# A two-layer decoder on one core: eight sequences in flight instead of seven, in shared tiles, and three projection biases moved from TensorE to GpSimd

## The chip, the cores and the metric

The kernel runs on one core of a Trainium2 chip. The time is the device time of one launch in microseconds (us), the median of several runs. Engines are named as the profile names them: PE is TensorE (PEld its weight loads), DVE is VectorE, ACT is ScalarE, POOL is GpSimd and SP is SyncE, which here only issues transfers. One execution is also recorded by the hardware profiler; its span runs from the first to the last instruction.

## The reference: what is computed

Sixteen independent sequences (B = 16) of 128 tokens with 256 features pass through two decoder layers. Each layer is self-attention, cross-attention and a feed-forward part, each followed by a layer norm. In short:

```python
x = layernorm(x + L0_attn(x))            # 16 heads, RoPE in a latent space of 32, causal softmax, c_proj + bias
x = layernorm(x + L0_xattn(ctx, x))      # linear attention: q @ (k^T v) * scale, then (.+x) layer norm with gamma, beta
x = layernorm(x + L0_ffn(x))             # FP4-quantised gate/up/down with silu, hidden 704
x = layernorm(x + L1_attn(x))            # causal softmax attention plus a second, moving-average term; proj + bias
x = layernorm(x + L1_xattn(x, ctx))      # masked softmax attention, Wo + bo, norm, relu MLP of 1024, norm
x = layernorm(x + L1_ffn(x))             # FP6-quantised linear layer + bias
```

Everything is float32. Three of these biases concern the change: that of c_proj in the first self-attention ("cproj"), bo in the second cross-attention ("x1o"), and that of the last linear layer ("f1"). Each is a row of 256 numbers that is added to every token's output.

## The kernel before

One sequence at a time fits all engines: its 128 tokens are the 128 partitions. The whole chain for one sequence is a Python generator, `stages(b, s)`, that runs `l0_attn`, `l0_xattn`, `l0_ffn`, `l1_attn`, `l1_xattn` and `l1_ffn` in turn. Here `b` is the sequence (an "entry") and `s = b % NS` is its slot. `NS = 7` slots exist, so seven entries are in flight at once; entry `b + 7` takes the slot of entry `b` when that is done. While the weights are being quantised, at the start, the last slot is lent to them (`quantised_weights`, released under "place"), and a few tiles of slots 4 and 5 hold start-up data.

Every slot has tiles of its own in SBUF, made by `mine(s, tag, ...)`: four large ones, A, B, C and D, used again and again by the steps of an entry; "yT" for transposed activations and for the sums ahead of a layer norm; and two "x" tiles that alternate (`turn`), for the running activations and, at first, the transposed input. Shared by all slots are the PSUM tiles: one group of four banks ("s", `quad`) for scores and four single banks ("p", `bank`), and the work tiles "e" (4), "t2" (3), "bd" (1), "silu", "fc" and others.

The order of instructions on every engine is fixed while the program is built, by a planner. Each generator yields what its next step needs: an engine, buffers and tiles. The class `Clock` keeps a modelled time per engine and tile, and at every turn of the last loop (`while runs`) the planner lists the entries whose next step could start within 0.05 us of the earliest. Of these it takes the one with the lowest key: entries that hold PSUM or work tiles first, then by the time at which the step became ready plus a constant `DELAY` of that entry, rounded to steps of 8 us, and then the older entry. Within a step, instructions are emitted to all engines that it uses, so each engine's queue is the planner's order. A transfer is issued by SP, in order, and waits in its queue until its tile is free.

When a PE step would start later than PE is free by at least `LEAST = 0.8` us, `Timed.fill` issues matmuls on constants ("filler", 128 x 512 in bf16), as many as fit into `SHARE = 0.75` of the gap, each counted as 0.222 us:

```python
        for _ in range(int(SHARE * gap / cost)):
            c.run("PE", bank, (), cost, 0.17)
            self._e.matmul(bank, lhsT=lhsT, rhs=rhs, start=True, stop=True)
```

A bias row is added on PE: `bias_row` multiplies a selecting matrix `sel` with a tile `bt` that holds the biases split into three bf16 terms, as the first matmul of an accumulation; `product` then adds the real matmuls. `out_proj` does a projection, and VectorE adds the residual x while it reads the PSUM bank. Sums of x and a row that a later step needs are made by GpSimd in `with_bias`, from `rows`, a tile in which a row is repeated in every partition. In the kernel before, this serves "x0b" and "be2".

All engine instructions are recorded in the profile under line 208 (a wrapper), fillers under line 161; so groups are told apart by tile names. For instance `ps_op_a<-bt,sel` is a bias row of an output projection, and `xb_be` is a sum made by `with_bias`.

Of the kernel before, what the change touches and what calls it, by code (L numbers as in the profile page):

```python
# [17 lines left out]
NS = 7  # L18
# [6 lines left out]
SHARE, LEAST = 0.75, 0.8  # L25

DELAY = (3.07, 2.06, 3.48, 0.32, 3.35, 1.80, 2.92, 0.82, 1.65, 1.28, 1.58, 3.49, 2.27, 4.62, 2.80, 1.07, 0.06)
# [9 lines left out]
    ("x0kv", 2 * D), ("cproj", D), ("a1p", D), ("x1o", D), ("x1b2", D), ("x1v", H * VW), ("f1", D), ("l2o", H * VW),  # L37
    ("x0g", D), ("x0b", D), ("g1", D), ("be1", D), ("g2", D), ("be2", D),
]
NADD = 3 * 512 + 2 * H * VW + D  # L40

BIASES = [
    ("x0kv", 0, 0, 512), ("cproj", 1, 0, D), ("a1p", 1, D, D), ("x1o", 2, 0, D), ("x1b2", 2, D, D),
    ("x1v", 3, 0, H * VW), ("f1", 3, H * VW, D),
]
NB = H * VW + D
# [167 lines left out]
def decoder_kernel(ctx: ExitStack, tc: tile.TileContext, a: dict, out: bass.AP):  # L214
# [13 lines left out]
    turns = {}  # L228

    def turn(name, n):  # L230
        turns[name] = turns.get(name, -1) + 1
        return turns[name] % n

# [18 lines left out]
    def mine(s, tag, shape, name, dtype=F32):  # L252

        return ring(own, f"{tag}{s}", 1, shape, dtype, name)
# [23 lines left out]
    def load_input(b):  # L278

        s = b % NS  # L280
        t = mine(s, f"x{turn(f'x{s}', 2)}_", [P, 2, P], f"xT_in_{b}")
        nc.sync.dma_start(out=t, in_=a["xT"][:, :, b * T : (b + 1) * T])
        if b < 3:
            clock.load(t, 8 * P)
        else:
            arrives(t)
        incoming[b] = t
# [22 lines left out]
    for g in range(4):  # L310
        n = 512 if g < 3 else NB
        nc.scalar.dma_start(
            out=brow[32 * g : 32 * g + 3, :n], in_=a["rows"][:, 512 * g : 512 * g + n].partition_broadcast(3)
        )
    clock.load(brow, 4 * 512 * 12 // P, True)
# [48 lines left out]
    sel = const.tile([P, 4, P], BF16, tag="sel", name="sel")  # L364
    V.tensor_copy(sel, group.unsqueeze(2).to_broadcast([P, 4, P]))
# [8 lines left out]
    for i in range(0, 5, 2):  # L374
        n = min(2, 5 - i)
        cm = wk.tile([P, 2, 64], F32, tag="bd", name="cm", bufs=1)
        GP.memset(cm, 0.0)
        GP.affine_select(
            out=cm, in_=cm, compare_op=ALU.is_ge, fill=-1e30, base=96 - 64 * i, pattern=[[-64, 2], [-1, 64]],
            channel_multiplier=1,  # L380
        )
        GP.tensor_copy(causal[:, i : i + n, :], cm[:, :n, :])
# [42 lines left out]
    l2o = own.tile([P, H * VW], F32, tag="B5", name="l2o")  # L425
# [91 lines left out]
    def new_x(b, s, name):  # L517

        k = turn(f"x{s}", 2)
        return mine(s, f"x{k}_", [P, D], f"x_{name}_{b}")  # L520
# [28 lines left out]
    def product(p, lhsT, weight, name):  # L549

        bias_row(p, name)
        n = lhsT.shape[1]
        for c in range(n):
            PE.matmul(p, lhsT=lhsT[:, c, :], rhs=weight[:, c, :], start=False, stop=(c == n - 1))
# [130 lines left out]
    def features(y, s, name):  # L685

        yT = mine(s, "yT", [P, 2, P], f"yT_{name}")
        yield from transposed(y, 2, yT, name)
        return yT

    def out_proj(yT, weight, bias, residual, s, name):

        yield "PE", "p", yT
        p = bank((D,), f"op_{name}")
        product(p, yT, weight, bias)
        yield "V", p
        h = mine(s, "yT", [P, D], f"h_{name}")
        V.tensor_tensor(h, p, residual, ALU.add)
        return h

# [54 lines left out]
    def fold_values():  # L755
        yield "PE", "p"
        t = bank((4, P), "fold_t")
        for kc in range(2):
            for oc in range(2):
                PE.transpose(t[:, 2 * kc + oc, :], raw_v[:, kc, oc * P : (oc + 1) * P], ident)  # L760
        yield "S", t
        vT = own.tile([P, 4, P], F32, tag="B4", name="fold_vT")
        S.copy(vT, t)
        yield "PE", "p"
        t = bank((P,), "fold_k")
        PE.transpose(t, w["w_kv2l"], ident)
        yield "S", t
        kT = own.tile([P, P], F32, tag="D4", name="fold_kT")
        S.copy(kT, t)
        yield "PE", "p"  # L770
        p = bank((4 * VW,), "fold_m")
        PE.matmul(p, lhsT=kT, rhs=raw_l2o, start=True, stop=True)
        yield "S", p

        m = own.tile([P, 8 * VW], F32, tag="A4", name="fold_md")
        GP.memset(m, 0.0)
        S.copy(m[:64, : 4 * VW], p[:64, :])
        S.copy(m[64:, 4 * VW :], p[64:, :])
        for kc in range(2):
            yield "PE", "p"  # L780
            p = bank((H * VW,), f"fold_w{kc}")
            for oc in range(2):
                PE.matmul(
                    p[:, oc * 8 * VW : (oc + 1) * 8 * VW], lhsT=vT[:, 2 * kc + oc, :], rhs=m, start=True, stop=True
                )
            yield "S", p
            S.copy(wv[:, kc, :], p)
        yield "PE", "p"
        p = bank((H * VW,), "fold_b")
        for oc in range(2):  # L790
            PE.matmul(
                p[:, oc * 8 * VW : (oc + 1) * 8 * VW], lhsT=col("qkv", 4 + oc).to_broadcast([P, P]), rhs=m,
                start=True, stop=False,
            )
            for i in range(2):
                at = (2 * oc + i) * 4 * VW
                PE.matmul(
                    p[:, at : at + 4 * VW], lhsT=col("kv2l").to_broadcast([P, P]), rhs=raw_l2o, start=False, stop=(i == 1)
                )
        yield "V", p  # L800
        V.tensor_tensor(l2o, p, l2o, ALU.add)
        yield from three_terms(bl, l2o, H * VW)
        release("wv", [bl, wv])
# [33 lines left out]
    def l0_attn(b, s):  # L837
# [13 lines left out]
        q = mine(s, "B", [P, 4, P], f"q0_{b}")  # L851
# [21 lines left out]
        yield "PE", "p", rot  # L873
        p = bank((4, P), f"qfk_{b}")
        PE.matmul(p, lhsT=w["w_wqk"], rhs=rot, start=True, stop=True)
        yield "S", p
        S.activation(q, p, AF.Identity, bias=wqk_b, scale=LAT**-0.5)
        ctx_ = context(b, s, "0")
# [5 lines left out]
        S.copy(v[:, : H * VW], p)  # L884
        y = yield from attention(b, s, q, k, v, None, f"a0_{b}", "A")
        yield "PE", "bt", y
        yT = yield from features(y, s, f"a0_{b}")
        h = yield from out_proj(yT, w["w_cproj"], "cproj", xs[b], s, f"a0_{b}")
# [5 lines left out]
    def l0_xattn(b, s, ctx_):  # L894
# [6 lines left out]
        xT = yield from features(xs[b], s, f"x0_{b}")  # L901
# [12 lines left out]
        yield "V", "bd", p2  # L914
        bd = work("bd", 1, [P, 2, P], f"bd_{b}")
# [6 lines left out]
        h = mine(s, "yT", [P, D], f"h_x0_{b}")  # L922
        V.tensor_tensor(h, p3.rearrange("p a b -> p (a b)"), xs[b], ALU.add)
        xb = with_bias(b, s, "x0b", "A")
        z = mine(s, "C", [P, D], f"z_x0_{b}")
# [59 lines left out]
    def l0_ffn(b, s):  # L985
# [3 lines left out]
        qT = yield from features(q, s, f"xq_{b}")  # L989
# [31 lines left out]
        r = mine(s, "yT", [P, D], f"h_f0_{b}")  # L1021
# [5 lines left out]
    def l1_attn(b, s):  # L1027
        xT = yield from features(xs[b], s, f"x1a_{b}")
# [3 lines left out]
        qa = mine(s, "A", [P, 2, P], f"a1qa_{b}")  # L1032
        ka = mine(s, "D", [P, 4, P], f"a1ka_{b}")
# [11 lines left out]
        project(p, w["w_a1k2"], xT)  # L1045
        yield "S", p
# [11 lines left out]
        ahead = mine(s, "yT", [P, D], f"ahead_{b}")  # L1058
# [46 lines left out]
        yT = mine(s, "yT", [P, 2, P], f"yT_a1_{b}")  # L1105
        S.copy(yT, p)
        h = yield from out_proj(yT, w["w_a1p"], "a1p", xs[b], s, f"a1_{b}")
# [5 lines left out]
    def l1_xattn(b, s, ctx_):  # L1113
# [25 lines left out]
        xT = yield from features(xs[b], s, f"x1_{b}")  # L1139
# [6 lines left out]
        yT = yield from features(y, s, f"x1y_{b}")  # L1146
        h = yield from out_proj(yT, w["w_x1o"], "x1o", xs[b], s, f"x1_{b}")
        t = mine(s, "C", [P, D], f"x1_{b}")
        yield from layernorm_affine(t, h, "g1", row("be1"), f"x1i_{b}")
        tT = yield from features(t, s, f"x1t_{b}")  # L1150
# [17 lines left out]
        h = mine(s, "yT", [P, D], f"h_ff_{b}")  # L1168
# [7 lines left out]
    def l1_ffn(b, s):  # L1176
        yield "V", xs[b]
        if b + NS < B:
            load_input(b + NS)
        q = mine(s, "D", [P, D], f"f1q_{b}")  # L1180
        yield from fp6(q, xs[b], D, f"f1_{b}")
        qT = yield from features(q, s, f"f1_{b}")
        h = yield from out_proj(qT, wf, "f1", xs[b], s, f"f1_{b}")
        y = mine(s, "C", [P, D], f"out_{b}")
        yield from layernorm(y, h, f"f1_{b}")
        nc.sync.dma_start(out=out[b], in_=y)
# [13 lines left out]
    places.update((tag, (tag, 1)) for tag in ("fc", "fC", "silu", "bd", "mT", "mi", "mb"))  # L1200
# [80 lines left out]
    while runs:  # L1281
        able = [(r.start(), r.age, r) for r in runs]
        able = [r for r in able if r[0] is not None]
        first = min(r[0] for r in able)


        at, _, run = min(
            (r for r in able if r[0] <= first + 0.05),
            key=lambda r: (not r[2].held, round((r[2].ready + DELAY[int(r[1]) if r[1] >= 0 else B]) / 8.0), r[1]),
        )  # L1290
        run.step(at)
        if run.need is None:
            runs.remove(run)
# [116 lines left out]
```

## Time and profile before

| | before |
|---|---|
| median of 3 runs | 985.59 us (984.91 to 986.45) |
| the profiled execution, its own time | 988.3 us |
| its span, first to last instruction | 986.6 us |
| mean granted TensorE clock | 0.983 |
| PE busy | 919.7 us, 11965 matmuls |
| DVE busy | 700.7 us |
| ACT busy | 508.8 us |
| POOL busy | 432.2 us |
| fillers on PE | 182, 44.5 us |

The page gives busy time by engine, the span in 40 slices of about 24.7 us (a digit is tenths of busy time; PEclk is the clock granted to TensorE, in tenths of full speed), groups of equal instructions with their number, total and mean time and the idle time of the engine ahead of them, and the waits. The mean of a PE instruction is a latency: matmuls are pipelined, and the next one starts before the last is out.

### The profile page before, as it was taken

How to read it: one execution, taken by the hardware profiler on the slowest of the kernel's cores; microseconds unless marked ns; L12 is line 12 of the kernel's file. 1: busy time of each engine (PE TensorE's matmuls, PEld its weight loads, DVE VectorE, ACT ScalarE, POOL GpSimd, SP SyncE). 2: the span in 40 equal slices, each digit the busy share in tenths (PEclk: the TensorE clock that was granted, in tenths of full speed). 3: DMA queues.
4: the chain of work that ended last, by engine and by line, in shares of the span. 5: the costliest groups of instructions: out<-in, count | busy, mean ns of one | idle time of the engine just before them, and what ended most of it. 6: DMA issues, size and time to landing. Idle time of an engine off the chain costs nothing.

```text
span 986.6 us, 28364 instructions
## 1 busy us (share of the span) xinstructions
PE 919.7 (93%) x11965; PEld 723.2 (73%) x11965; DVE 700.7 (71%) x1440; ACT 508.8 (52%) x1113; POOL 432.2 (44%) x898
## 2 busy tenths in 40 slices
PE   7889899999899999999999999999998899999996
PEld 6566567777678878788777787878776687686764
DVE  5999999976764666659596967957666458963544
ACT  3244445665556444655546666555555545555432
POOL 3335523644435344445363464435434435344321
PEclk9899999999999989999999999999999999999998
DMA  8910000000000000000000000000000000000000
GB/s 230 210 45 7 28 7 7 11 9 20 5 23 12 19 25 21 23 22 17 18 18 16 21 13 7 24 1 23 21 13 25 8 11 7 14 13 15 10 7 12
DMA packets 47864, 25.57 MB, mean 26 GB/s; under 512 B 23004, under 2 KB 45516, under 8 KB 47480
## 3 DMA queue, kind: packets, MB, share of 16 engines
q1 hardware_dynamic: 46816, 22.39, 8.3%
q8 instruction: 94, 1.54, 0.6%
q0 software_dynamic: 192, 0.93, 0.4%
q10 hardware_dynamic: 728, 0.44, 0.1%
q14 instruction: 34, 0.28, 0.1%
HBM read 19.57 MB, written 2.10 MB: 22 GB/s over the span
## 4 chain that ended last, share of the span: by engine, by line
PE 55%; DVE 26%; ACT 8%; POOL 6%; issue 4%; DMA 0%; ACTq 0%; POOLq 0%; DVEq 0%
PE ps_ff L208 10%; PE ps_s_a L208 3%; PE ps_dn L208 3%; PE ps_st_a L208 3%; DVE nm_a L208 3%; DVE rope L208 2%; PE ps_op_a L208 2%; PE ps_x0kv L208 2%; PE ps_pg L208 2%; PE ps_pu L208 2%; PE ps_a1qk L208 2%; PE ps_yt L208 2%; DVE hh L208 2%; PE ps_qk L208 2%; PE ps_st_x L208 2%
## 5 line engine op out<-in xcount | busy, mean ns | idle before, releaser
L208 POOL TENSOR_SCALAR_AFFINE_SELECT e_a<-e_a 128x1024 f32<-128x1024 f32 x64 | 76.0, 1190 | 88.9 <-ACT e_a L208 88.7
L208 DVE TENSOR_REDUCE nm_a<-ps_s_a 128x16 f32<-128x2048 f32 x32 | 73.1, 2286 | 28.4 <-PE ps_s_a L208 28.2
L208 ACT ACTIVATE e_a<-ps_st_a 128x1024 f32<-128x1024 f32 x64 | 65.7, 1030 | 27.1 <-PE ps_st_a L208 26.9
L208 PE MATMUL ps_ff<-yT_x1t,w 128*128 128x128 f32 x512 | 63.1, 277 | 1.0 <-ACT yT_x1t L208 1.0
L208 PEld LDWEIGHTS ps_ff<-yT_x1t,w 128*128 128x128 f32 x512 | 60.1, 192 | 4.4 <-issue 2.1
L208 PE MATMUL ps_ff<-w,ff 128*128 128x256 f32 x256 | 61.0, 381 | 0.0
L208 ACT ACT_TABLE_LOAD x41 | 52.6, 1283 | 12.8 <-DMA brow<-in_rows_dram 9.0
L208 POOL CAST maxima<-nm_a 128x16 bf16<-128x16 f32 x32 | 8.9, 279 | 98.8 <-DVE nm_a L208 98.8
L208 PEld LDWEIGHTS ps_ff<-w,ff 128*128 128x128 f32 x256 | 46.2, 190 | 7.7 <-ACT ff L208 1.0
L208 ACT ACTIVATE ff<-ps_ff,cols 128x128 f32<-128x128 f32 x128 | 36.5, 369 | 27.1 <-PE ps_ff L208 27.0
L208 PE MATMUL ps_dn<-qw_down,hT 128*128 128x256 f32 x192 | 47.2, 383 | 0.7 <-ACT hT L208 0.5
L208 PE MATMUL ps_pg<-gu,yT_xq 128*128 128x352 f32 x128 | 44.7, 471 | 0.7 <-DVE hh L208 0.4
L208 DVE TENSOR_REDUCE nm_x<-ps_s_x 128x16 f32<-128x2048 f32 x16 | 36.5, 2282 | 11.4 <-PE ps_s_x L208 11.1
L161 PE MATMUL ps_filler<-ones,ident_b 128*128 128x512 bf16 x182 | 44.5, 383 | 0.0
L208 PE MATMUL ps_pu<-gu,yT_xq 128*128 128x352 f32 x128 | 43.2, 460 | 0.6 <-DVE bd L208 0.6
L208 PE MATMUL ps_yp_a<-e_a,v_a 128*32 128x128 f32 x1024 | 36.5, 281 | 3.6 <-POOL e_a L208 2.3
L208 ACT ACTIVATE e_x<-ps_st_x 128x1024 f32<-128x1024 f32 x32 | 31.8, 1026 | 13.7 <-PE ps_st_x L208 13.7
L208 PEld LDWEIGHTS ps_dn<-qw_down,hT 128*128 128x128 f32 x192 | 34.4, 190 | 5.6 <-ACT hT L208 0.7
L208 POOL TENSOR_SCALAR_AFFINE_SELECT maT<-maT 128x1024 f32<-128x1024 f32 x16 | 18.0, 1123 | 42.0 <-ACT maT L208 42.0
L208 ACT ACTIVATE x_x<-z_x,rstd_x 128x256 f32<-128x256 f32 x32 | 19.3, 604 | 31.7 <-POOL rstd_x L208 26.8
L208 ACT ACTIVATE x_a<-h_a,rstd_a 128x256 f32<-128x256 f32 x32 | 19.4, 605 | 31.4 <-POOL rstd_a L208 29.9
L208 PEld LDWEIGHTS ps_yp_a<-e_a,v_a 128*32 128x32 f32 x1024 | 26.3, 111 | 12.0 <-issue 4.8
(367 smaller groups left out, 2659.2 us busy)
## 6 DMA issues: line engine op xcount, KB each, us to landing
ctx<-in_ctxT_dram SPq DMA_DIRECT2D x32, 128.0 KB
xT_in<-in_xT_dram SPq DMA_DIRECT2D x16, 128.0 KB
w<-in_w_dram SPq DMA_DIRECT2D x2, 1024.0 KB
x_in<-in_x_dram SPq DMA_DIRECT2D x16, 128.0 KB
out_dram<-out SPq DMA_DIRECT2D x16, 128.0 KB
ahead<-x_f SPq DMA_DIRECT2D x16, 127.0 KB
mi<-in_mask_dram SPq DMA_DIRECT2D x16, 64.0 KB
rows<-in_rows_dram POOLq DMA_DIRECT2D x1, 768.0 KB, 5.5
```

The source lines that it names most:

```text
L161: self._e.matmul(bank, lhsT=lhsT, rhs=rhs, start=True, stop=True)
L208: return f(*args, **kw)
```

## The change

`NS` becomes 8. To make room for eight sets of tiles, "yT", the second "x" tile and the shared "bd" go: the input lands in B, transposed activations and sums go to whichever of A to D is free at that step (`features` and `out_proj` now take the tag), `ahead` takes the second half of the tile that holds `qa`. In `l0_attn` the product for v is done ahead of the one with `w_wqk`, since q is to take the place of the transposed input. The slots lent at the start change with it (slot 7 for the weights, slot 6 for `fold_values`).

The biases of "cproj", "x1o" and "f1" leave `bt` and join `rows`. `with_bias` adds each to x on GpSimd in the step ahead of the projection; `out_proj_onto` does the projection without a bias row, and VectorE adds PSUM onto that sum in place. The bias "a1p" stays on PE.

In the planner, `LEAST` becomes 1.4, the `DELAY` values are smaller (0.04 to 0.56), and the key is rounded to 2 us instead of 8.

```diff
-NS = 7
+NS = 8
...
-SHARE, LEAST = 0.75, 0.8
-
-DELAY = (3.07, 2.06, 3.48, 0.32, 3.35, 1.80, 2.92, 0.82, 1.65, 1.28, 1.58, 3.49, 2.27, 4.62, 2.80, 1.07, 0.06)
+SHARE, LEAST = 0.75, 1.4
+
+DELAY = (0.04, 0.26, 0.15, 0.27, 0.15, 0.52, 0.34, 0.45, 0.56, 0.30, 0.28, 0.08, 0.47, 0.04, 0.22, 0.10, 0.51)
...
-    ("x0kv", 2 * D), ("cproj", D), ("a1p", D), ("x1o", D), ("x1b2", D), ("x1v", H * VW), ("f1", D), ("l2o", H * VW),
+    ("x0kv", 2 * D), ("a1p", D), ("x1b2", D), ("x1v", H * VW), ("l2o", H * VW), ("cproj", D), ("x1o", D), ("f1", D),
     ("x0g", D), ("x0b", D), ("g1", D), ("be1", D), ("g2", D), ("be2", D),
 ]
-NADD = 3 * 512 + 2 * H * VW + D
+NADD = 2 * 512 + 2 * H * VW
...
     def load_input(b):
 
         s = b % NS
-        t = mine(s, f"x{turn(f'x{s}', 2)}_", [P, 2, P], f"xT_in_{b}")
+        t = mine(s, "B", [P, 2, P], f"xT_in_{b}")
...
     def new_x(b, s, name):
 
-        k = turn(f"x{s}", 2)
-        return mine(s, f"x{k}_", [P, D], f"x_{name}_{b}")
+        return mine(s, "x", [P, D], f"x_{name}_{b}")
...
-        bias_row(p, name)
+        if name is not None:
+            bias_row(p, name)
...
+    def out_proj_onto(h, yT, weight, name):
+
+        yield "PE", "p", yT, h
+        p = bank((D,), f"op_{name}")
+        product(p, yT, weight, None)
+        yield "V", p, h
+        V.tensor_tensor(h, p, h, ALU.add)
...
-        yield "PE", "p", rot
-        p = bank((4, P), f"qfk_{b}")
-        PE.matmul(p, lhsT=w["w_wqk"], rhs=rot, start=True, stop=True)
-        yield "S", p
-        S.activation(q, p, AF.Identity, bias=wqk_b, scale=LAT**-0.5)
-        ctx_ = context(b, s, "0")
         yield "PE", "p", "wv", xT
         p = bank((H * VW,), f"v0_{b}")
         product(p, xT, wv, "l2o")
         yield "S", p
         v = values(s, f"a0_{b}")
         S.copy(v[:, : H * VW], p)
+        yield "PE", "p", rot
+        p = bank((4, P), f"qfk_{b}")
+        PE.matmul(p, lhsT=w["w_wqk"], rhs=rot, start=True, stop=True)
+        q = mine(s, "B", [P, 4, P], f"q0_{b}")
+        ctx_ = context(b, s, "0")
+        yield "S", p
+        S.activation(q, p, AF.Identity, bias=wqk_b, scale=LAT**-0.5)
         y = yield from attention(b, s, q, k, v, None, f"a0_{b}", "A")
         yield "PE", "bt", y
-        yT = yield from features(y, s, f"a0_{b}")
-        h = yield from out_proj(yT, w["w_cproj"], "cproj", xs[b], s, f"a0_{b}")
+        yT = yield from features(y, s, "B", f"a0_{b}")
+        h = with_bias(b, s, "cproj", "C")
+        yield from out_proj_onto(h, yT, w["w_cproj"], f"a0_{b}")
...
-        yield "V", "bd", p2
-        bd = work("bd", 1, [P, 2, P], f"bd_{b}")
+        yield "V", p2
+        bd = mine(s, "D", [P, 2, P], f"bd_{b}")
...
-        qa = mine(s, "A", [P, 2, P], f"a1qa_{b}")
-        ka = mine(s, "D", [P, 4, P], f"a1ka_{b}")
+        both = mine(s, "A", [P, 4, P], f"a1qa_{b}")
+        qa, ahead = both[:, 0:2, :], both[:, 2:4, :].rearrange("p a b -> p (a b)")
...
-        yT = yield from features(y, s, f"x1y_{b}")
-        h = yield from out_proj(yT, w["w_x1o"], "x1o", xs[b], s, f"x1_{b}")
+        yT = yield from features(y, s, "B", f"x1y_{b}")
+        h = with_bias(b, s, "x1o", "D")
+        yield from out_proj_onto(h, yT, w["w_x1o"], f"x1_{b}")
...
-        qT = yield from features(q, s, f"f1_{b}")
-        h = yield from out_proj(qT, wf, "f1", xs[b], s, f"f1_{b}")
+        qT = yield from features(q, s, "A", f"f1_{b}")
+        h = with_bias(b, s, "f1", "D")
+        yield from out_proj_onto(h, qT, wf, f"f1_{b}")
...
-            key=lambda r: (not r[2].held, round((r[2].ready + DELAY[int(r[1]) if r[1] >= 0 else B]) / 8.0), r[1]),
+            key=lambda r: (not r[2].held, round((r[2].ready + DELAY[int(r[1]) if r[1] >= 0 else B]) / 2.0), r[1]),
```

## The prediction

> **What bounds the kernel now.** I read the page's busy shares first, then its row of slices, then the groups of instructions, then the timeline of TensorE where it pauses, then the windows around the places where its clock falls.
>
> ```profile
> PE 919.7 (93%) x11965; PEld 723.2 (73%) x11965; DVE 700.7 (71%) x1440; ACT 508.8 (52%) x1113; POOL 432.2 (44%) x898
> ...
> PE   7889899999899999999999999999998899999996
> PEclk9899999999999989999999999999999999999998
> ```
>
> The page says that TensorE (PE) is busy 93% of the span and nothing else comes near over the whole of it. But part of this PE work is no work: `fill` issues matmuls that only keep the array going while the plan sees nothing ready. In the groups, shapes kept apart:
>
> ```profile
> L161 PE MATMUL ps_filler<-ones,ident_b 128*128 128x512 bf16 x182 | 44.5, 383 | 0.0
> ...
> L208 POOL TENSOR_TENSOR xb_be<-x_a,rows 128x256 f32<-128x256 f32 x16 | 13.6, 847 | 0.0
> ...
> L208 PE MATMUL ps_op_a<-bt,sel 128*128 128x256 bf16 x32 | 8.8, 275 | 0.2
> ...
> L208 DVE TENSOR_TENSOR h_x<-ps_op_x,x_a 128x256 f32<-128x256 f32 x16 | 6.6, 414 | 8.4 <-PE ps_op_x L208 8.4
> ```
>
> Fillers take 44.5 us, and PE is idle for 986.6 - 919.7 = 66.9 us besides. So about 111 us of the span are not PE's own work, and 875 are. That 111 is what an eighth entry can reach; the 875 can only shrink by the bias rows. The timeline of PE at the two longest pauses shows both what a filler is and what a bias row costs:
>
> ```profile
> 955.45 0.27 PE L208 MATMUL ps_op_x<-bt,sel 128*128 128x256 bf16 x1
> 955.56 1.03 PE L208 MATMUL ps_op_x<-w_x1o,yT_x1y 128*128 128x256 f32 x4
> 956.42 2.97 PE L161 MATMUL ps_filler<-ones,ident_b 128*128 128x512 bf16 x13
> 959.94 0.41 PE L208 MATMUL ps_tr_x1t<-ident,x 128*128 128x128 f32 x2 [0.55 <-DVE x L208]
> ...
> 969.29 6.64 PE L161 MATMUL ps_filler<-ones,ident_b 128*128 128x512 bf16 x30
> 978.55 0.41 PE L208 MATMUL ps_tr_f<-ident,f1q 128*128 128x128 f32 x2 [2.62 <-DVE f1q L208]
> ```
>
> After each run of fillers PE still waits for VectorE (0.55 and 2.62 us). So taking fillers out saves nothing by itself; what saves is that the gap behind them is not there. And a run measures its gap: `fill` issues the whole part of 0.75 x gap / 0.222, so n fillers stand for n x 0.296 to (n + 1) x 0.296 us. For 13 that is 3.8 to 4.1 us, where the trace has 959.94 - 956.42 = 3.5; for 30 it is 8.9 to 9.2, where the trace has 9.3. The plan's gaps are there on the chip.
>
> **The change, part by part.**
>
> *Bias rows off PE.* The row's mean of 275 ns is a latency under which the next matmul already runs: 955.45 to 955.56 is 0.11 us from start to start. 48 of the 64 rows in output projections go (16 each for cproj, x1o and f1; a1p stays): 48 x 0.11 = **5.3 us** off PE. Their 48 weight loads (`sel`) overlap matmuls.
>
> *The adds on POOL.* 48 more adds of x and a row, the form of xb_be:
>
> ```profile
> L208 POOL TENSOR_TENSOR xb_be<-x_a,rows x16: 722/730/1418, 302.9 to 960.9; 128x256 f32<-128x256 f32 x16
> L208 DVE SCALAR_TENSOR_TENSOR z_x<-h_ff,rstd_x1j,xb_be x16: 452/484/1487, 315.5 to 970.9; 128x256 f32<-128x256 f32 x16
> its engine sat idle before it (us, times) until:
>   POOL rstd_x1j L208: 8.0, 9
> ```
>
> 48 x 0.73 = 35 us (41 at the mean of 0.85), POOL from 432 to about 470 of 986. The reader of such an add waits for rstd, never for the add. The Trainium skill's GPSIMD Engine Reference, section Engine selection, speaks against this place: a two-input elementwise add belongs on VectorE, being about 2x slower on GpSimd. The rows agree on the size (730 against 414 ns), but here no add leaves VectorE: its add of PSUM and x only changes its second operand. By the rule the price would be 35 us if all of it lay on the path; by the row, where 16 such adds hold nobody up, it is zero. What differs: the add is issued in the step that copies yT, so it has only the two transfers of PE's projection (about 1 us) to finish in, and VectorE's add then waits for it. Queued behind that add on VectorE is what comes next there, a maximum over scores for instance, for which POOL's maxima, PE's transpose and a softmax wait. Bounds 0 and 35; I take **+2**.
>
> *Gaps, from eight entries and the finer sort* (2 us in place of 8). The built programs' instruction orders hold 182 fillers in 28 runs before and 97 in 10 runs after. By stage (before the 800th PE matmul, the middle, the last 900): 71, 22 and 89 before; 46, 0 and 51 after. In us, with half a step more for each run: 182 x 0.296 + 28 x 0.148 = 58.0 before, 97 x 0.296 + 10 x 0.148 = 30.2 after. Not all of the difference is real, because gaps from 0.8 to 1.4 us are no longer filled and so no longer seen. Before there were 14 runs of two to four fillers, about 1.05 us each, 14.7 in all; after, there may be none or as many. I take half, 7. Gain 58.0 - 30.2 - 7 = **20.8 us**, ends 13 and 28.
>
> *The clock.* Fewer fillers can let the clock fall. The windows around two falls:
>
> ```profile
> 346.00:349.50 3.50, 1.71 (x12) 0.95 (x14) 3.36 (x6) 1.91 (x5) 2.93 (x6) 1.00 0.05 15
> 349.50:352.90 3.40, 3.40 (x54) 2.89 (x55) 2.20 (x4) 0.72 (x2) 2.14 (x3) 0.50 0.06 19
> ...
> 748.90:752.30 3.40, 1.63 (x23) 1.25 (x27) 3.26 (x8) 2.34 (x5) 1.28 (x2) 1.00 0.00 0
> 752.30:755.70 3.40, 3.40 (x43) 3.04 (x40) 2.46 (x7) 1.69 (x4) 1.30 (x4) 0.50 0.00 0
> ```
>
> Third column is PE's busy time, the third from last the granted clock. A stretch of 3.4 us in which PE worked half the time is followed by one at 0.50. The Trainium skill, TensorE: Matmul & The Clock Gate, section "HAM oscillation", gives the rule as no idle gaps above about 3.4 us; by it, unfilled gaps of at most 1.4 us cost nothing. The trace differs: no single idle there was that long (PE stood 1.44 us ahead of 349.09, after shorter idles), and the clock fell. Two or three gaps of a microsecond close together are enough, so fewer fillers have a price: 3.4 x 0.5 = 1.7 us per fall. I take two more falls, **+3.4** (0 to 7).
>
> *Costed at nothing.* (a) l0_attn now does the v product ahead of the wqk matmul, since q shares tile B with the transposed input: q comes some 1.03 us later in each entry, under the other entries' work. Without that cover it would be 16 x 1.03 = 16. (b) SP's queue issues as many transfers as before, now into shared tiles: x_in waits for the slot's last reader, the POOL add for f1, and could hold a later `ahead` behind it. The waits of the trace have only two for a DMA, 7.2 and 9.0 us, both at the very start; x_in is needed only at cproj, a whole attention later. Zero, up to 2. (c) The broadcast `rows` grow by 0.39 MB, which is 1.7 us of the 230 GB/s of the first slices, behind the transfers that are waited for: 0, up to 1.7. (d) `bd` leaves its single shared buffer, for which PE once waited 0.6 us.
>
> Sum: -5.3 + 2 - 20.8 + 3.4 = -20.7. The profiled execution took 988.3 us (span 986.6), 2.7 above the median of 985.6: 988.3 - 20.7 = 967.6, which as a median is **965**. With the ends of gaps, clock and adds (0 to 10) it is 955 to 979.
>
> **The rivals.** *The gaps stay, only unfilled.* From 74 to 172 us VectorE, not PE, is the bound: 23.0 to 23.8 us of each slice of 24.6, with the weights' quantisation on it, and an eighth entry gives it more to do, not less. Then only the bias rows come out: 985.6 - 5.3 = 980, and a little more if the end gains. For it: after each filler run PE waited for VectorE. Against it: 22 fillers vanish in the middle and 38 at the end, where VectorE has room (8 to 16 us of 24.6).
>
> *POOL's queue becomes the path (slower).* POOL runs in order and sits long behind its own waits: 98.8 us over 32 times until VectorE's maxima, 88.7 over 43 until ScalarE's exponentials, up to 9.3 at once. An add that falls behind such a wait holds VectorE's add, and with it all that is queued on VectorE. If each of the 48 passes 0.75 us on to PE, that is +36 against -26 of gaps and bias rows, and with the clock 985.6 + 36 - 26 + 3.4 = 999. It decides from 0.47 us per add (22.7 / 48). Against it: POOL is idle 56% of the span, and eight entries give PE other work while one waits.
>
> **How the numbers follow.** The first forecast gets 0.63, the unfilled gaps 0.17, POOL's queue and its like 0.20. About 0.2% (2 us) can be told from no change. The first is faster nearly throughout; of the second a quarter falls within 2 us or above. So faster 0.77, same 0.05, slower 0.18. The range of 8 in 10 goes from 950 (gaps at their best with no falls of the clock) to 989, which takes in the second case and leaves most of the third out.
>
> **What would show it.** Right: fillers at about 97 with 22 to 30 us busy, none between 250 and 850 us; the groups of ps_op_f and ps_op_x without a bias row; xb_cproj, xb_x1o and xb_f near 730 ns with VectorE's add behind them waiting for PE, not POOL; PE's idle no larger than 67 us; mean granted clock 0.975 to 0.985. The forecast is wrong if PE's idle grows by the 20 us that the fillers lose, if waits of VectorE for xb_ tiles pass 20 us, or if the clock falls under 0.97.

## The result and the profile after

The changed kernel takes 988.29 us (median of 13 executions, 986.57 to 992.98) against 985.59 us (13 executions, 982.94 to 989.80): a ratio of 1.0034, interval 1.0017 to 1.0051. It is 0.3% slower, about 3.4 us by the ratio, where 20 us less were forecast. In what follows a difference in us is a difference of two such ratios times 985.6, so that kernels measured beside different executions of the kernel before can be compared. Each such difference is uncertain by about 2 to 3 us.

The page of the profiled execution after (987.65 us, span 985.7), its busy line and its slices:

```profile
PE 897.6 (91%) x11829; PEld 716.9 (73%) x11832; DVE 707.1 (72%) x1440; ACT 506.7 (51%) x1113; POOL 467.2 (47%) x946
...
PE   6787888989899999999899999899999999999896
...
PEclk9999999999999999999999999999999999999998
```

and its groups, shapes kept apart, for the fillers and the sums made on GpSimd:

```profile
L160 PE MATMUL ps_filler<-ones,ident_b 128*128 128x512 bf16 x97 | 23.2, 386 | 0.0
...
L207 POOL TENSOR_TENSOR xb_cproj<-x_in,rows 128x256 f32<-128x256 f32 x16 | 13.2, 826 | 0.0
...
L207 POOL TENSOR_TENSOR xb_f<-x_x,rows 128x256 f32<-128x256 f32 x16 | 11.8, 738 | 18.6 <-PE ps_tr_f L207 14.4 <-issue 2.5 <-DVE st_x L207 1.7
L207 POOL TENSOR_TENSOR xb_x1o<-x_a,rows 128x256 f32<-128x256 f32 x16 | 11.8, 739 | 0.0
```

The change did what its text says. The fillers are 97 in 23.2 us; the three sums are there, at the forecast length (medians of 727 to 733 ns), 36.8 us in all on POOL. PE is busy 22.1 us less. But its idle time has grown from 66.9 to 985.7 - 897.6 = 88.1 us, by 21.2, which the prediction had named as the sign of its failure. Fillers and idle together were 111.4 us before and are 23.2 + 88.1 = 111.3 us after. Over the whole span not one microsecond of the 111 that the eighth entry was to reach has gone. By stage, in the two traces (idle and filler time of PE together, in us):

| stage | before | after |
|---|---|---|
| 0 to 75 us | 24.3 | 25.7 |
| 75 to 250 us | 18.2 | 25.7 |
| 250 to 885 us | 34.4 | 31.9 |
| 885 us to the end | 34.5 | 28.0 |

The middle and the end did gain, 9 us together, and the first 250 us lost as much, although fillers became fewer there too (71 to 46).

Where the pauses grew is shown by two windows. First the kernel before, then the kernel after; the columns are the busy time (and instructions) of PE, PEld, DVE, ACT and POOL, then the granted clock.

```profile
core 0: us, PE busy (x) PEld busy (x) DVE busy (x) ACT busy (x) POOL busy (x), PEclk, DMA share, GB/s
75.00:170.00 95.00, 88.45 (x1046) 61.19 (x1045) 91.05 (x193) 41.94 (x87) 40.38 (x72) 1.00 0.05 13
170.00:250.00 80.00, 77.11 (x955) 60.09 (x954) 62.90 (x132) 51.95 (x106) 42.80 (x88) 0.98 0.05 13
```

```profile
core 0: us, PE busy (x) PEld busy (x) DVE busy (x) ACT busy (x) POOL busy (x), PEclk, DMA share, GB/s
75.00:170.00 95.00, 79.76 (x1077) 56.46 (x1080) 87.42 (x179) 40.30 (x81) 45.44 (x79) 0.96 0.04 13
170.00:250.00 80.00, 72.86 (x785) 56.22 (x780) 66.66 (x146) 46.02 (x94) 42.97 (x83) 1.00 0.03 9
```

From 75 to 250 us PE loses 165.6 - 152.6 = 13 us of busy time, of which 8.8 - 3.3 = 5.5 are fillers and 7.5 its own work, while VectorE's sum is 154 us in both. Counted as stretches of at least 0.8 us from the modelled end of PE's own work to its next start, these 175 us hold 11.6 us of pauses before and 19.5 after; in the last 100 us they fall from 20.7 to 18.1. The timeline of PE after shows what those pauses are; the bracket gives the idle time ahead and what ended it:

```profile
89.04 0.48 PE L207 MATMUL ps_lat<-qk,w_q2l 32*64 32x128 f32 x16 [1.50 <-ACT e_a L207]
...
97.43 0.48 PE L207 MATMUL ps_lat<-qk,w_q2l 32*64 32x128 f32 x16 [2.91 <-DVE rope L207]
...
114.67 0.44 PE L207 MATMUL ps_s_a<-causal,ident_b 32*32 32x512 bf16 x16 [1.63 <-DVE rope L207]
120.10 0.44 PE L207 MATMUL ps_s_a<-causal,ident_b 32*32 32x512 bf16 x16 [1.45 <-DVE nm_a L207]
...
131.79 0.50 PE L207 MATMUL ps_st_a<-q,k 32*128 32x128 f32 x8 [1.38 <-ACT e_a L207]
...
155.34 0.22 PE L207 MATMUL ps_tm_a<-ident_b,maxima 128*128 128x128 bf16 x1 [0.74 <-DVE hh L207]
...
165.75 0.44 PE L207 MATMUL ps_tr_x<-ident,x_a 128*128 128x128 f32 x2 [1.53 <-DVE hh L207]
```

Five of these seven wait for VectorE, the longest among them; two wait for ScalarE's exponentials. No filler stands in front of any: a filler needs a gap of `LEAST` in the plan, and a PSUM bank to spare. Which of the two was missing is not on record. The chain of waits says the same; first before, then after:

```profile
PE 55%; DVE 26%; ACT 8%; POOL 6%; issue 4%; DMA 0%; ACTq 0%; POOLq 0%; DVEq 0%
```

```profile
PE 45%; DVE 37%; ACT 6%; POOL 5%; issue 5%; DMA 2%; SPq 0%; ACTq 0%; POOLq 0%; DVEq 0%
```

### The profile page after: what moved, and what is told of

Same layout as the page of the kernel before. It is cut to its first block, busy times and chain, and to the rows that moved or that the text cites. A ratio compares the mean times of both kernels' runs of the same rounds, so it can differ in the third digit from the quotient of the medians.

```text
span 985.7 us, 28116 instructions
## 1 busy us (share of the span) xinstructions
PE 897.6 (91%) x11829; PEld 716.9 (73%) x11832; DVE 707.1 (72%) x1440; ACT 506.7 (51%) x1113; POOL 467.2 (47%) x946
## 4 chain that ended last, share of the span: by engine, by line
PE 45%; DVE 37%; ACT 6%; POOL 5%; issue 5%; DMA 2%; SPq 0%; ACTq 0%; POOLq 0%; DVEq 0%
PE ps_ff L207 10%; DVE hh L207 5%; DVE rope L207 3%; DVE nm_a L207 3%; PE ps_st_x L207 2%; PE ps_a1qk L207 2%; PE ps_s_a L207 2%; PE ps_st_a L207 2%; PE ps_op_a L207 2%; PE ps_dn L207 2%; DVE xq L207 2%; PE ps_yt L207 2%; PE ps_op_f L207 1%; DVE fc_h L207 1%; DVE f1q L207 1%
## 5 line engine op out<-in xcount | busy, mean ns | idle before, releaser
L207 POOL CAST maxima<-nm_a 128x16 bf16<-128x16 f32 x32 | 11.6, 363 | 75.1 <-DVE nm_a L207 75.1
L207 ACT ACTIVATE e_x<-ps_st_x 128x1024 f32<-128x1024 f32 x32 | 31.9, 1025 | 16.9 <-PE ps_st_x L207 16.9
L207 ACT ACTIVATE x_x<-z_x,rstd_x 128x256 f32<-128x256 f32 x32 | 19.4, 608 | 33.7 <-POOL rstd_x L207 29.5
L207 POOL TENSOR_TENSOR rot<-rope,rope 128x512 f32<-128x512 f32 x16 | 21.3, 1334 | 27.9 <-DVE rope L207 27.9
L207 PE MATMUL ps_qk<-xT_in,w_qkv 128*128 128x128 f32 x256 | 34.5, 296 | 0.0
L207 PEld LDWEIGHTS ps_pu<-gu,yT_xq 128*128 128x128 f32 x128 | 24.3, 190 | 13.5
```

What stands on the lines that cost most here:

```text
L207: return f(*args, **kw)
```

## The experiments

"Order held" means that the sequence of the planner's steps and the place of every filler are written out as a list taken from the kernel named, so that an edit cannot make the planner choose another order. Three theories were on record: A, the adds on GpSimd ate the gain; B, the order of eight entries bunches VectorE's work; C, no planned order runs on the chip as planned. S, the larger broadcast of `rows` delays the start, came later.

**The three biases back on PE** (after, order held):

```diff
-        h = with_bias(b, s, "cproj", "C")
-        yield from out_proj_onto(h, yT, w["w_cproj"], f"a0_{b}")
+        h = yield from out_proj(yT, w["w_cproj"], s, "C", f"a0_{b}", "cproj", xs[b])
```

and likewise for x1o and f1, with the old `ROWS` and `sel`.

> The changed kernel with its order of steps and its fillers held exactly, but the three biases back on TensorE as bias rows (48 rows of 0.11 us) and the 48 GpSimd adds gone; VectorE adds PSUM and x as before the change. Theory A (the adds are what ate the gain: they stretch VectorE's instructions that read two SBUF tensors and stand in POOL's queue): at or under 984 us, VectorE busy back from 707 to about 701. Theory B (the order of eight entries puts VectorE-heavy steps together, the adds are small): 988 to 993, up to the 5.3 us of the rows slower than the changed kernel. Theory C (no order runs as planned, whatever is added): as B.

Measured: 982.09 us, ratio 0.9964 (0.9948 to 0.9980), 3.5 us faster than before and 6.9 faster than after. It beats both kernels: eight entries in shared tiles, in this planned order, gain, and the move of the biases loses more than that. Its busy line:

```profile
PE 896.9 (92%) x11877; PEld 714.6 (73%) x11880; DVE 703.3 (72%) x1440; ACT 506.5 (52%) x1113; POOL 430.4 (44%) x898
```

With a span of 979.7 us and fillers of 24.2, PE's idle and filler time is 82.8 + 24.2 = 107.0 us, 4.4 less than before: with the rows on PE the pauses did shrink, by a fifth of the forecast.

**A later add, with no wait for a shared tile** (after, order held). The sums `xb_be` and `xb_f` had begun to wait on POOL until PE let go of a shared tile.

```diff
-        xb = with_bias(b, s, "be2", "B")
...
+        xb = with_bias(b, s, "be2", "B")   # one step later
         h = mine(s, "A", [P, D], f"h_ff_{b}")
...
-        h = with_bias(b, s, "f1", "D")
+        h = with_bias(b, s, "f1", "C")
...
-        y = mine(s, "C", [P, D], f"out_{b}")
+        y = mine(s, "D", [P, D], f"out_{b}")
```

> The changed kernel with its order of steps held, but the two adds that wait for a shared tile no longer do: the add for be2 (tile B, until then read by the matmuls of ps_ff; POOL stood 24.6 us in 7 waits) is issued one step later, when those are done, and the add for f1 goes to tile C instead of D (POOL stood 14.4 us for ps_tr_f), the output to D. Theory A: 3 to 8 us faster than the changed kernel (980 to 985), since POOL no longer holds what is queued behind. Theories B and C: within 2 us of it (986 to 990), since POOL has 50% to spare.

Measured: 994.38 us, ratio 1.0083 (1.0057 to 1.0109): a miss, 4.8 us slower than after. The waits on POOL, first after and then in this kernel:

```profile
POOL maxima L207 <- DVE nm_a L207: 75.1, 29, 5.2
...
POOL xb_be L207 <- PE ps_ff L207: 24.6, 7, 9.1
...
POOL xb_f L207 <- PE ps_tr_f L207: 14.4, 8, 5.5
```

```profile
POOL maxima L206 <- DVE nm_a L206: 94.4, 31, 10.3
...
POOL xb_be L206 <- PE ps_ff L206: 7.9, 2, 4.5
```

The wait for `ps_ff` fell from 24.6 to 7.9 us and that for `ps_tr_f` left, and nothing was gained: POOL stands instead at the maxima, where VectorE's `nm_a` is late. So taking out the new waits of 24.6 and 14.4 us, the first thing that catches the eye in the profile after, gave no time back. The edit also moves an add and exchanges two tiles, so this run alone does not show that the waits cost nothing. Why this kernel is slower was not settled; its mean granted clock was lower (0.978 against 0.982).

**The planner's constants exchanged.** Both kernels, replanned with the other's `LEAST`, `DELAY` and rounding (2 or 8 us).

> The kernel before (seven entries, old tiles, biases on TensorE) with only the planner's constants of the change: LEAST 1.4, the small DELAY values, sort in steps of 2 us; the order is planned anew and has 157 fillers. Theory B: the finer sort alone brings VectorE-heavy steps together: 992 to 1005, with longer stretches of VectorE near 95% busy. Theory C: 990 to 1010, from an order that was not chosen for this kernel, without a pattern in VectorE. By the filler count alone (157 against 182, as the prediction read it): 980 to 986.

> The changed kernel (eight entries, shared tiles, adds on GpSimd) with the planner's constants of before: LEAST 0.8, the large DELAY values, sort in steps of 8 us; planned anew, 176 fillers. Theory B: if the fine sort was at fault, 975 to 984. Theory C: 985 to 1000. By the filler count alone (176 against 182, less the rows): 978 to 984.

Measured: seven entries with the new constants 1014.51 us (1.0286, 1.0257 to 1.0315), slower than any of the three ranges expected; eight entries with the old ones 996.05 us (1.0092, 1.0065 to 1.0119). Each kernel is faster with its own set of constants, and another order, with its fillers, moves the time by 6 to 28 us. What the new constants do is thus no separate term of a sum: with seven entries they cost 28 us.

**The broadcast of `rows` split** (after, order held): the three new rows, 384 KB, go behind the last weights.

```diff
-    nc.gpsimd.dma_start(out=rows, in_=a["rows"][:, NADD:].partition_broadcast(P))
+    nc.gpsimd.dma_start(out=rows[:, 3 * D :], in_=a["rows"][:, NADD + 3 * D :].partition_broadcast(P))
...
+    nc.sync.dma_start(out=rows[:, : 3 * D], in_=a["rows"][:, NADD : NADD + 3 * D].partition_broadcast(P))
```

> The changed kernel, order held, with the broadcast of rows split: the part that was there before (768 KB) stays where it was, the three new rows (384 KB) are issued by SP behind the last weights. Theory S (the larger broadcast, landing in 7.1 us instead of 5.5, delays the first inputs and weights, and the whole chain behind them by 2 to 4 us): 984 to 986.5. If the start has nothing to do with it: 987.5 to 989.

Measured: 986.41 us, ratio 1.0023 (1.0007 to 1.0039). That is just inside the range of S, but the intervals overlap: 1.1 us less than after, with 2 us of uncertainty, so a small cost of the broadcast is neither shown nor excluded. The start itself does not speak for S. PE's timeline before, after, and in this kernel:

```profile
11.46 2.36 PE L208 MATMUL ps_biases<-cols,dense 128*128 128x2 f32 x20
```

```profile
11.45 4.27 PE L207 MATMUL ps_biases<-cols,dense 128*128 128x2 f32 x20
```

```profile
11.86 4.26 PE L206 MATMUL ps_biases<-cols,dense 128*128 128x2 f32 x20
```

The same 20 matmuls take 4.26 us here too, with the small broadcast in front. In other kernels with the large one they took 2.29. So these 2 us, by which PE's work starts later in the profile after, are not shown to be the broadcast's doing; they appear in kernels of both sorts.

**The three biases left out** (after, order held): no bias row, no add and no larger broadcast for cproj, x1o and f1. The expectation says the rest.

> The changed kernel, order held, with the three biases left out altogether: neither bias rows on TensorE nor adds on GpSimd, small rows. Against the version with bias rows (982.1) it lacks 48 x 0.11 = 5.3 us of TensorE. If TensorE's work is the bound, as the prediction took it: 976 to 978. If TensorE waits on chains most of the time, so that its work is not what counts: 980 to 983.

Measured: 981.57 us, ratio 0.9953 (0.9934 to 0.9972). Against the kernel with bias rows on PE that is 1.1 us by the ratios, with overlapping intervals, for 48 x 0.11 = 5.3 us of PE work. In the two traces the rows do take that much ahead of the first real matmul (0.11 us each, 5.4 in all), although PE's busy sum differs by only 1.2 us.

**The adds alone, with nobody waiting.** The same kernel, with an add on GpSimd where each of the 48 stood:

```diff
+    def scrap_add(b):
+        GP.tensor_tensor(scrap, xs[b], row("x0b"), ALU.add)
...
+        scrap_add(b)
         h = yield from out_proj(yT, w["w_cproj"], s, "C", f"a0_{b}", "cproj", xs[b])
```

> After, the order of all steps and the fillers held as they were. The three biases are left out of the result; in the place of each of the 48 GpSimd adds stands an add of the same size (x and another row, 128x256), written to one scrap tile that nobody reads, and VectorE adds PSUM and x. So it is the kernel without the three biases (981.6 us) plus 48 adds on GpSimd for which no engine waits and which wait for no shared tile; the larger broadcast at the start is not there. Theory A1 (the adds cost by their dependencies: VectorE, or PE after it, waits for the sum or the add waits for a tile): 981 to 983 us. Theory A2 (they cost by being there: they lengthen VectorE's instructions that run beside them, and take turns on GpSimd's queue): 985 to 987 us, with VectorE's busy sum 4 us or more above that of the kernel without the biases, and the two-input instructions longer when GpSimd runs.

Measured: 987.32 us, ratio 1.0014 (1.0003 to 1.0024): 6.0 us more than without the adds. The busy lines, first without and then with them:

```profile
PE 895.7 (91%) x11829; PEld 714.2 (73%) x11832; DVE 703.0 (72%) x1440; ACT 506.5 (52%) x1113; POOL 431.2 (44%) x898
```

```profile
PE 895.9 (91%) x11832; PEld 714.2 (73%) x11832; DVE 709.5 (72%) x1440; ACT 507.2 (52%) x1113; POOL 468.8 (48%) x946
```

No instruction reads the scrap tile and none of the adds waits for a shared one, and yet three quarters of the 8.0 us between the kernel without the biases and after are there (A2). VectorE, whose instructions are the same 1440, is busy 6.5 us longer. Paired one by one in the two traces, the 74 VectorE instructions that run beside a scrap add are 7.0 us longer in sum, and the other 1366 together 0.3 us shorter. The lengthening is uneven: 19 of the 74 are longer by 0.1 us or more, up to 0.56, and most of the others hardly change. The largest case, first without and then with the adds (two products of h; the second of them is the one that grew, from 0.89 to 1.45):

```profile
217.82 1.83 DVE L207 TENSOR_TENSOR hh<-hh,fc_h 128x704 f32<-128x704 f32 x2
```

```profile
214.20 2.39 DVE L207 TENSOR_TENSOR hh<-hh,fc_h 128x704 f32<-128x704 f32 x2
...
215.11 0.72 POOL L207 TENSOR_TENSOR scrap<-x_in,rows 128x256 f32<-128x256 f32 x1
```

**Less VectorE work** (both kernels, order held): the two instructions that round h to its grid, 704 columns each, are left out for every entry.

```diff
-        V.tensor_tensor(xn, xn, st, ALU.add)
-        V.tensor_tensor(xn, xn, st, ALU.subtract)
+        if width != FF:
+            V.tensor_tensor(xn, xn, st, ALU.add)
+            V.tensor_tensor(xn, xn, st, ALU.subtract)
```

> The kernel before, order and fillers held, with two VectorE instructions per entry left out: the add and subtract that round h to the grid in the FP4 step of 704 columns (16 x 2 x 0.98 = 31 us of VectorE). If VectorE counts little with seven entries: 980 to 985.5. If it sets the pace: 965 to 975.

> The changed kernel, order and fillers held, with the same two VectorE instructions per entry left out (31 us of VectorE). Theory B (with eight entries in this order VectorE has become the pace-maker in stretches): 12 to 20 us faster than the changed kernel, 968 to 976, and clearly more than the same cut gives before. Otherwise the same few us as before, 982 to 987.

Measured: 975.27 us (0.9889, 0.9868 to 0.9910) and 975.96 us (0.9896, 0.9873 to 0.9918). The busy lines, before and after, each without the two instructions:

```profile
PE 908.6 (93%) x11965; PEld 715.0 (73%) x11965; DVE 667.6 (69%) x1408; ACT 507.8 (52%) x1113; POOL 419.6 (43%) x898
```

```profile
PE 889.5 (91%) x11829; PEld 710.8 (73%) x11832; DVE 677.6 (70%) x1408; ACT 505.8 (52%) x1113; POOL 459.0 (47%) x946
```

VectorE's busy time fell by 33.1 and 29.5 us, and the time by 10.9 and 13.6: a third to a half of each microsecond. Here an instruction on VectorE is dear, and it was so before the change as well; theory B, as something new with eight entries, is not borne out by so small a difference. The edit also takes two instructions of about 1 us out of each entry's chain, and the runs do not separate the engine's time from the chain's.

**No fillers** (both kernels, order held; `fills = {}`).

> After, the order of all steps held, with none of the 97 fillers. Theory G (a run of fillers stands in a pause that is really there, as the prediction read them): no gain, PE's idle time up by about the 23 us of the fillers, and the clock lower by at most four falls of 1.7 us: 988 to 995 us. Theory H (the plan is off by up to 10 us from the chip, so fillers stand where PE has work and hold it up): faster, down to 980 us.

> Before, the order of all steps held, with none of the 182 fillers (44.5 us busy in 28 runs). Theory G (fillers stand in real pauses): no gain, PE's idle time up by about 44 us, and the clock lower by up to eight falls of 1.7 us: 986 to 1000 us. Theory H (fillers hold PE's work up): faster, 970 to 983 us; then the pauses that the prediction wanted to close were in part the fillers' own.

Measured: 995.62 us (1.0096, 1.0067 to 1.0125) after and 998.60 us (1.0131, 1.0113 to 1.0149) before. The clock row of the second shows why, at its end above all, where most fillers had stood:

```profile
PEclk9889899999899999999999999999999999999787
```

On balance fillers hold nothing up (theory G, not H): without them both kernels are slower, at a lower clock. I had allowed too few falls. The busy lines, after and before, without fillers (spans 988.9 and 996.7):

```profile
PE 882.6 (89%) x11735; PEld 710.9 (72%) x11735; DVE 706.8 (71%) x1440; ACT 506.8 (51%) x1113; POOL 468.0 (47%) x946
```

```profile
PE 899.3 (90%) x11783; PEld 720.4 (72%) x11783; DVE 698.9 (70%) x1440; ACT 508.4 (51%) x1113; POOL 430.4 (43%) x898
```

PE's idle time rose by 18.2 and 30.5 us, less than the 23.2 and 44.5 of the fillers: PE's own work, slower, takes up part of the pauses. Whether some fillers also held a little work up is not separated. The mean granted clock over all timed executions went from 0.9907 to 0.9574 before, and from 0.9816 to 0.9623 after. If the clock is all that the fillers change, that prices it: 12.9 us for 0.0333, and 6.1 us for 0.0193, so 0.32 to 0.39 us for each thousandth.

## Why the prediction was wrong

The sum was -5.3 (bias rows) + 2 (adds) - 20.8 (gaps) + 3.4 (clock) = -20.7. With the runs it reads -1.1 (bias rows) + 8.0 (adds, and what came with them) - 5.7 (gaps) + 2.2 (clock, without what the adds take of it) = +3.4. Every term of this is uncertain by 2 us or more.

- **Gaps, the largest error.** The prediction said "a run measures its gap", and took the gain from a count of fillers. Where a filler stands, that is true: at the end of the kernel after, the timeline still has runs with a wait for VectorE behind them, as the prediction read it before.

```profile
964.54 4.70 PE L160 MATMUL ps_filler<-ones,ident_b 128*128 128x512 bf16 x21
971.30 0.44 PE L207 MATMUL ps_tr_f<-ident,f1q 128*128 128x128 f32 x2 [2.06 <-DVE f1q L207]
```

  The failed step is the converse: that a gap without a filler is no gap. Of the forecast's gaps, 7 us were set aside for those below the new `LEAST`; the pauses of 1.4 to 2.9 us from 75 to 170 us are at or above it on the chip, and still unfilled. From 75 to 250 us fillers fell from 36 to 14 and idle and filler time rose by 7.5 us; at the end, where they fell from 84 to 51, it fell by 6.5. The term is worked out as what is left: the kernel without the three biases is 4.6 us faster than before, of which its lower clock takes 6.1 thousandths x 0.36 (the middle of the two prices) = 2.2 and the missing rows give 1.1, so -4.6 - 2.2 + 1.1 = -5.7, a remainder that agrees with the 4.4 us counted in the trace of the kernel with bias rows on PE.
- **Bias rows: the premise.** "The 875 can only shrink by the bias rows" took PE's busy time for its bound. Taking 5.3 us of PE work away was worth 1.1 us, with an uncertainty of 2.4, so less than its full length. The Trainium skill, Perfetto Trace Analysis, section Identifying the Most-Contended Engine, says that the busy share of matmuls is not a good measure of how close the engine is to its limit, because matmuls are pipelined, and to use weight loads' busy share, and the share of peak FLOPs, instead. Here the two busy shares are 93% and 73%; by the second PE stands about level with VectorE, which the page shows at 71%. The runs agree that the 93% was no bound: 0.2 us of time for each microsecond of PE work, against a third to a half for VectorE, though the uncertainty leaves open which of the two is dearer. I read the 93% and did not test it against VectorE's row by stage, although I had named 74 to 172 us as VectorE's in the first rival.
- **Adds on GpSimd: the mechanism, and the size.** The rows gave the right length, and no wait for the sums appeared. The prediction priced an add only by who would wait for it (nobody by the row of `xb_be`, VectorE's add for the 2 us taken); the adds cost 6.0 us with nobody waiting. The failed step is that an add beside VectorE's work was put at nothing. The Trainium skill's GPSIMD Engine Reference, table of Specifications, says that GpSimd shares its SBUF interfaces with VectorE and contends with VectorE's instructions that have two SBUF inputs or run in a 2-port mode. The prediction had weighed another rule of this page. Worked out from the trace without the biases, VectorE's `xq<-xq,fc_x` takes 0.42 us when GpSimd rests and 0.62 on average (median 0.44) when GpSimd works beside most of it, while the reduction `nm_a`, which reads PSUM, takes 2.28 us either way. Beside the scrap adds some instructions with one input grew too (`fc_f<-fc_f`, once from 0.29 to 0.71 us), so two inputs are not needed for it here; no run shows which mode these ran in. By the worth of VectorE's time found above, 6.5 us of it make 2 to 3 of the 6.0; the clock, lower by 2.8 thousandths, makes about 1. The rest, 2 to 3 us, is not separated: the adds also take turns in POOL's queue.
- **What came with the adds** (the larger broadcast, waits for shared tiles, VectorE's one wait of 1.0 us at a sum) makes the other 2.0 of the 8.0 us, with overlapping intervals. I had put the broadcast at 0 to 1.7, and nothing here contradicts that.
- **The clock** was about right in size. Over the timed executions the mean is 0.9816 after against 0.9907 before: 9.1 thousandths, or 3.3 us, where 3.4 were forecast. It was right by luck. A fall of 3.41 us to half speed is 1.73 thousandths of the mean, so 9.1 are about five more falls, not two; and at 0.36 us a thousandth each cost about 0.6 us, not 1.7, because PE's work was not the bound. The two errors cancel. And the profiled execution of before had 0.983, below every one of the 27 executions of it (0.985 to 0.994) that ran beside the first experiments.
- **(a), (b) and (d), costed at nothing,** were not tried one by one. The kernel with bias rows on PE has all three and is faster than before, so together they cost less than the gaps gain.
- **The rivals.** The first, gaps that stay unfilled because VectorE is the bound from 74 to 172 us, had the mechanism of the larger error, and its "a little more if the end gains" is what the stages show; its 980 us still held the bias rows at their full 5.3, and had no price for the adds. The second had the sign. It named GpSimd, but by a wait of VectorE for the sums at 0.75 us each; the cost is 6.0 / 48 = 0.13 us each, below the 0.47 from which it was to decide, and it decided because the gain in front of it (gaps and bias rows) was about 7 us, not 26.

## What to carry to other kernels

A filler counts a pause that the plan sees and can fill, so fewer fillers can mean fewer pauses or only fewer that are filled; before taking a pause as closed, add PE's idle and filler time (111 us here, before and after) and read each stage's windows for the engine that ends the waits. A high busy share of PE is no bound until removing a little of its work moves the time: hold the order, leave out enough of one engine's work to stand clear of the noise, and compare what a microsecond is worth on each. Moving work to an engine that looks idle is priced not only by who waits for it, but by what it slows beside it.

## What the runs showed of the hardware

- An add of 128x256 f32 on GpSimd cost about 0.13 us of this kernel's time (6.0 us by 48) even though nothing depended on it, and the VectorE instructions beside such adds grew by 7.0 us in all. A single one can more than double: `fc_f<-fc_f` from 0.29 to 0.71 us. GpSimd's other work does the same: in the kernels with and without the scrap adds the longest `xq<-xq,fc_x` takes 1.26 us instead of 0.42, and stands both times beside the same 1.10 us of GpSimd's `e_a<-e_a`.
- The granted clock falls to half in stretches of 3.41 us or two to four times that (6.83 to 13.65), apart from the last stretch of a run; the mean over an execution of the kernel before ran from 0.985 to 0.996. A thousandth of the mean granted clock was worth 0.32 to 0.39 us here; if PE's work were the bound, the estimate would be 0.99.
- In the first 20 us the same group of 20 matmuls took 2.29 to 4.27 us while the record gave a clock of 1.00, in kernels of both sorts. The Trainium skill, TensorE: Matmul & The Clock Gate, section on the HAM clock gate, says that the warm-up varies between runs because the activity window runs free; that would be a stretch at a lower clock, which the record does not show here, so the cause of the 2 us stays open.
